# A perceiver block on one core: query weights averaged a head at a time, and a new order of the opening

## The chip, the core and the metric

The kernel runs on one core of one Trainium2 chip. A core has a matrix engine (TensorE, "PE" in the profile; its weight loads are the row "PEld"), a vector engine (DVE), a scalar engine (ACT), GpSimd (POOL) and a synchronisation engine (SP), which here issues nearly all transfers. Each engine takes its own instructions in order, and engines wait for each other through semaphores. TensorE writes to PSUM, a small accumulation memory; the rest of the data lies in SBUF. The metric is the device time of one execution in microseconds, the median of several runs.

## What is computed

A block of three residual layers works on x of shape 32 x 64 x 512 in float32. The change touches only the first layer, cross attention: x is normalised, projected to queries of four heads of 128, rotated by position, and attends to a masked memory of 32 x 1601 x 512 with one shared head of keys and values.

```python
xn = _rmsnorm(_layernorm(x), rms_scale)
mn = _rmsnorm(ctx_1024, rms_scale)
q = einsum('BTD,NDH->BTNH', xn, q_w)
k, v = einsum('BSD,cKDH->cBSKH', mn, kv_w)
q = rope(q, S + arange(T)) * 128 ** -0.5
k = rope(k, arange(S))
probs = softmax(where(mask, q . k, -2.4e38))
x = x + einsum('BTNH,NHD->BTD', probs . v, out_w)
# then causal self attention of 16 heads, and a feed-forward of 2048
```

## The kernel before

**Tiling.** The 2048 tokens are four groups of four tiles of 128 (`GROUPS`, `GQ = 512`). Width 512 is four chunks of 128 (`DC`). A query of group g and head h (`query`, L229) is four products over the chunks, weights `wq[:, c, h]` against the transposed x of the group (`wide(g)`, from the host array `xT`), 512 tokens wide, into one PSUM bank. In float32 each product is two matmul instructions in the profile, so a query has eight.

**How the layer norm is taken out of the product.** The weights are scaled by 1 + rms_scale (`scale1`), and their mean over the width is subtracted; the mean is itself a product with a matrix `each` (scale1 / 512 on all columns). So raw x can be multiplied. The missing standard deviation of each token comes from `spread_of` (L196, statistics of a 128x512 tile of tokens that `fetch_raw` loads), `deviations` (L203, a power on POOL) and `diagonals` (L211, ACT writes four scaled identities into `eye`). `tables(g)` (L222) multiplies ones by `eye` into a PSUM tile `rb` and on DVE makes the group's cosine and sine tables with the deviations in them. `rotate_query` (L234) then takes two ACT copies and three DVE operations of 128x512 and writes `qT_all`.

**The opening (L263 to L379).** It holds group 0 entirely, the statistics and tables of group 1, the means and centring of the query weights (`wmean`, L324 to L348), the scaling of `wkv`, and a ranking of the sequences by how much of their memory is unmasked: the mask ends and a small table come in one transfer `opening`; `mf` is their cast, `count` two products, `halves`, `need`, `key`, `mine`, `rank`, `here` small DVE operations, `placed` four tiny products, and `ints` holds the order and a flag `fits`. `keep_busy(n)` issues n products of ones that nobody reads. `in_order` (L145) ties the instructions of each engine, SP included, to the order in which they are written.

**After the branch on `fits` (L381, L628).** All engines read the flag, so nothing behind it starts before `ints` is written. The common way, `cross_last`, interleaves the queries of groups 1 to 3 (`query_steps`, L244) with the loads of the memory in ranked order (`load_rows`, `load_rest`), with tokens and x of groups 2 and 3, and from group 2 on with the key and value products of pair 0 (`project`, L517, tile `kvp`). PSUM for queries alternates: even heads take a pool of two banks `ps_lg`, odd heads one of two `ps_pt`. Tiles are shared in place: `wide(g)` has two buffers for four groups, `fetch_raw` one buffer for all, so a load waits until the group before has been read. After the queries a loop over pairs of sequences does projection, logits, softmax and output.

Of the kernel before, what the change touches and what calls it, by code (L numbers as in the profile page):

```python
# [18 lines left out]
F32 = mybir.dt.float32  # L19
# [61 lines left out]
def perceiver_kernel(ctx: ExitStack, tc: tile.TileContext, a: dict, out: bass.AP):  # L81
# [83 lines left out]
    turned_probs = wo.rearrange("p h (k q) -> p (h k) q", q=P)  # L165
    ints = const.tile([1, B + 1], I32, name="ints")

    wq = wo.rearrange("p c (h k) -> p c h k", h=NH)
    scale1 = const.tile([P, DC], F32, name="scale1")


# [14 lines left out]
    def fetch_wide(g, queues):  # L186
        for k, queue in enumerate(queues):
            part = slice(k * DC // len(queues), (k + 1) * DC // len(queues))
            queue.dma_start(wide(g)[:, part], a["xT"][:, g, part])
# [27 lines left out]
    def fetch_rotations(pool):  # L217
        qrot = pool.tile([P, 2, T], F32, name="qrot")
        nc.sync.dma_start(qrot, a["qrot"])
        return qrot  # L220
# [8 lines left out]
    def query(g, h, ps):  # L229
        for c in range(DC):  # L230
            nc.tensor.matmul(ps, wq[:, c, h, :], wide(g)[:, c], start=(c == 0), stop=(c == DC - 1))  # L231
        return ps

    def rotate_query(g, h, ps):  # L234

        t = norm.tile([P, D], F32, tag="xn", name=f"qt_{g}_{h}")
        nc.scalar.copy(t[:H], ps[H:])
        nc.scalar.copy(t[H:], ps[:H])
        t = t.rearrange("p (b t) -> p b t", t=T)
        nc.vector.tensor_tensor(turn, ps.rearrange("p (b t) -> p b t", t=T), cosr, ALU.mult)  # L240
        nc.vector.tensor_tensor(t, t, sinr, ALU.mult)
        nc.vector.tensor_tensor(qT_all[:, S8 * g : S8 * (g + 1), h, :], turn, t, ALU.add)

    def query_steps(qrot, psq, psr):  # L244

        for g in range(1, GROUPS):
            more = g + 1 < GROUPS
            for h in range(NH):
                q = query(g, h, psq(h, f"q_{g}_{h}"))
                if h == 0 and g > 1:  # L250
                    tables(g, qrot, psr(f"rb_{g}"))
                rotate_query(g, h, q)
                if more and h < 2:
                    spread_of(g + 1, 2 * h)
                    spread_of(g + 1, 2 * h + 1)
                if more and h == 1:
                    deviations(g + 1)
                if more and h == 2:
                    diagonals(g + 1)
                yield g, h  # L260


    with ExitStack() as st:  # L263
        r1 = st.enter_context(tc.tile_pool(name="r1", bufs=1))
        ps_q = [
            st.enter_context(tc.tile_pool(name=f"ps_q{k}", bufs=2, space=PSUM)) for k in range(2)
        ]
        ps_b = st.enter_context(tc.tile_pool(name="ps_b", bufs=2, space=PSUM))
        ps_r = st.enter_context(tc.tile_pool(name="ps_r", bufs=2, space=PSUM))


        CUTS = np.cumsum([0, B * NC, 4 * B * 5, 4 * 2 * NC])
        opening = r1.tile([P, CUTS[-1]], U8, name="opening")
        m8, table, steps = (opening[:, i:j] for i, j in zip(CUTS, CUTS[1:]))
        table = table[:B].bitcast(F32).rearrange("p (k b) -> p k b", b=B)
        steps = steps[:B].bitcast(F32).rearrange("p (k c) -> p k c", c=NC)

        begin = len(nc.cur_bb.bb.instructions)


        def keep_busy(n):
            idle = ps_b.tile([P, P], F32, tag="b", name=f"idle_{n}")
            for _ in range(n):
                nc.tensor.matmul(idle, ones, ones, start=True, stop=True)

        nc.sync.dma_start(opening, a["opening"])
        nc.scalar.dma_start(scale1, a["rms"])
        for k in (0, 2):
            nc.sync.dma_start(wo[:, k : k + 2], a["wq"][:, k : k + 2])
        keep_busy(5)  # L290
        mf = r1.tile([P, B, NC], F32, name="mf")
        nc.vector.tensor_copy(mf.rearrange("p b c -> p (b c)"), m8)
        nc.vector.tensor_scalar(scale1, scale1, 1.0, None, ALU.add)
        each = r1.tile([P, DC, P], F32, name="each")
        nc.scalar.activation(
            each, scale1.unsqueeze(2).to_broadcast([P, DC, P]), AF.Copy, scale=1.0 / D
        )
        fetch_wide(0, [nc.sync, nc.sync])
        fetch_raw(0)
        qrot = fetch_rotations(r1)  # L300
        nc.sync.dma_start(wkv, a["wkv"])


        halves = r1.tile([B, B, 2, NC], F32, name="halves")
        for k in range(2):
            part = slice(k * T, (k + 1) * T)
            count = ps_r.tile([P, B, NC], F32, tag="r", name=f"count_{k}")
            nc.tensor.matmul(
                count[:B].rearrange("p b c -> p (b c)"),
                ones[part, :B],  # L310
                mf[part].rearrange("p b c -> p (b c)"),
                start=True,
                stop=True,
            )
            nc.vector.scalar_tensor_tensor(
                halves[:, :, k],
                count[:B],
                0.0,
                steps[:, k].unsqueeze(1).to_broadcast([B, B, NC]),
                ALU.is_gt,  # L320
                ALU.mult,
            )
        keep_busy(4)
        wmean = ps_b.tile([P, D], F32, tag="b", name="wmean")  # L324
        for c in range(DC):
            nc.tensor.matmul(wmean, each[:, c], wo[:, c], start=(c == 0), stop=(c == DC - 1))
        need = r1.tile([B, B], F32, name="need")
        nc.vector.tensor_reduce(need, halves.rearrange("p b k c -> p b (k c)"), AX.X, ALU.max)

        key = r1.tile([B, B], F32, name="key")  # L330
        nc.vector.scalar_tensor_tensor(key, need, float(B), table[:, 0], ALU.mult, ALU.add)
        own = r1.tile([B, B], F32, name="own")
        nc.vector.tensor_tensor(own, key, table[:, 1], ALU.mult)
        mine = r1.tile([B, 1], F32, name="mine")
        nc.vector.tensor_reduce(mine, own, AX.X, ALU.add)
        above = r1.tile([B, B], F32, name="above")
        nc.vector.tensor_scalar(above, key, mine, None, ALU.is_gt)
        rank = r1.tile([B, 1], F32, name="rank")
        nc.vector.tensor_reduce(rank, above, AX.X, ALU.add)
        here = r1.tile([B, B], F32, name="here")  # L340
        nc.vector.tensor_scalar(here, table[:, 2], rank, None, ALU.is_equal)
        placed = ps_r.tile([P, 2, B], F32, tag="r", name="placed")
        nc.tensor.matmul(placed[:1, 0], mine, here, start=True, stop=True)
        nc.tensor.matmul(placed[:1, 1], table[:, 3, 0:1], here, start=True, stop=True)
        for c in range(DC):
            nc.vector.scalar_tensor_tensor(  # L346
                wo[:, c], wo[:, c], scale1[:, c : c + 1], wmean, ALU.mult, ALU.subtract
            )  # L348
        heads = [ps_q[h % 2].tile([P, GQ], F32, tag="q", name=f"q_0_{h}") for h in range(NH)]
        query(0, 0, heads[0])  # L350

        fit2 = r1.tile([1, 2, B], F32, name="fit2")
        nc.vector.tensor_tensor(fit2[:, 0], placed[:1, 0], table[:1, 4], ALU.is_lt)
        nc.vector.tensor_scalar(fit2[:, 1], placed[:1, 0], float(B), None, ALU.is_ge)
        fit = r1.tile([1, 1], F32, name="fit")
        nc.vector.tensor_reduce(fit, fit2.rearrange("p k b -> p (k b)"), AX.X, ALU.min)
        nc.vector.tensor_copy(ints[:, :B], placed[:1, 1])
        nc.vector.tensor_copy(ints[:, B:], fit)
        for k in range(4):
            spread_of(0, k)  # L360
        deviations(0)
        diagonals(0)
        for c in range(DC):
            nc.scalar.activation(wkv[:, c], wkv[:, c], AF.Copy, scale=scale1[:, c : c + 1])
        query(0, 1, heads[1])
        fetch_raw(1)
        fetch_wide(1, [nc.sync])
        for k in range(4):
            spread_of(1, k)
        deviations(1)  # L370
        query(0, 2, heads[2])
        tables(0, qrot, ps_b.tile([P, GQ], F32, tag="b", name="rb_0"))
        query(0, 3, heads[3])
        for h in range(NH):
            rotate_query(0, h, heads[h])
            if h == 1:
                diagonals(1)
        tables(1, qrot, ps_b.tile([P, GQ], F32, tag="b", name="rb_1"))
        in_order(begin, (Engine.PE, Engine.DVE, Engine.Activation, Engine.Pool, Engine.SP))  # L379

    fits = nc.values_load(  # L381
# [1338 lines left out]
```

## Time and profile before

| what | value |
|---|---|
| median of 3 runs | 900.34 us (899.08 to 900.46) |
| profiled execution | 899.0 us |
| its span | 896.1 us |
| TensorE busy | 881.9 us, 98% |
| VectorE busy | 626.9 us, 70% |
| ScalarE busy | 377.6 us, 42% |
| first query starts | 10.63 us |
| first query of group 1 starts | 27.5 us |
| first `kvp` product starts | 45.6 us |

The profile is one execution. The span runs from its first to its last recorded instruction; what lies around it is 2.9 us. The page gives busy times by engine, the busy share in forty slices, the chain of work that ended last, groups of instructions by line and shape, and transfers with their time from issue to landing. The timeline lists instructions by start, with the idle time of the engine before them and who ended it in brackets. A busy TensorE is not necessarily one at its peak, since matmuls are pipelined.

### The profile page before, as it was taken

The numbers are of one execution on the slowest core, as the hardware profiler recorded it, in microseconds if no ns is written. First come the engines' busy times: TensorE is split into PE (matmuls) and PEld (weight loads), VectorE is DVE, ScalarE is ACT, GpSimd is POOL, SyncE is SP. The second block draws the span as 40 slices with busy tenths as digits, with TensorE's granted clock in tenths as the row PEclk, the third lists the DMA queues.
The fourth block names the chain that finished last, engine by engine and source line by source line (L and its number), as shares of the span: only waits on it lengthen the run. The fifth ranks groups of instructions, "written<-read, shape, count | busy, mean of one in ns | idle before, by whom it ended". The sixth has DMA issues, their size and how long they took to land.

```text
span 896.1 us, 12923 instructions
## 1 busy us (share of the span) xinstructions
PE 881.9 (98%) x4536; PEld 635.0 (71%) x4536; DVE 626.9 (70%) x1198; ACT 377.6 (42%) x811; POOL 67.3 (8%) x79
## 2 busy tenths in 40 slices
PE   9999999999999999999999999999999999999997
PEld 4456777777778767667666766676668878788885
DVE  5975656455655671688889888885776886876864
ACT  2554545545555431222222323224554554555550
POOL 0110111111101100000000000000001000010000
PEclk9999999999999999999999999999999999999999
DMA  8975898775685342011111100100000020010101
GB/s 267 318 250 182 233 250 261 222 248 159 198 257 157 101 161 101 1 59 40 44 37 48 35 25 25 36 12 1 1 1 1 1 47 1 7 42 1 32 16 52
DMA packets 58723, 88.05 MB, mean 98 GB/s; under 512 B 10516, under 2 KB 30872, under 8 KB 58264
## 3 DMA queue, kind: packets, MB, share of 16 engines
q1 hardware_dynamic: 57888, 86.58, 32.1%
q8 instruction: 38, 0.62, 0.3%
q10 hardware_dynamic: 760, 0.55, 0.2%
q14 instruction: 37, 0.30, 0.1%
HBM read 78.72 MB, written 4.19 MB: 93 GB/s over the span
## 4 chain that ended last, share of the span: by engine, by line
PE 86%; DVE 9%; ACT 2%; issue 1%; DMA 1%; POOL 0%; POOLq 0%; ACTq 0%
PE y L1530 13%; PE kvp L523 13%; PE fh L1179 11%; PE xo L649 6%; PE aV L1268 5%; PE aWQ L1256 5%; PE aWK L1256 5%; PE aout L1377 5%; PE q L231 5%; PE lgp L565 3%; PE enc L633 3%; PE pt L618 2%; PE sc L1311 1%; PE aptp L1350 1%; PE po L1363 1%; DVE s L1316 1%
## 5 line engine op out<-in xcount | busy, mean ns | idle before, releaser
L523 PE MATMUL kvp<-wkv,ct 128*128 128x256 f32 x576 | 134.7, 379 | 0.0
L523 PEld LDWEIGHTS kvp<-wkv,ct 128*128 128x128 f32 x576 | 107.0, 190 | 21.6 <-issue 8.8
L1530 PE MATMUL y<-wp,hTh 128*128 128x512 f32 x236 | 94.4, 400 | 0.4 <-DVE xres L1507 0.4
L1530 PE MATMUL y<-wp,hTl 128*128 128x512 f32 x236 | 92.8, 393 | 0.0
L1179 PE MATMUL fh<-fxh,wf 128*128 128x512 f32 x256 | 71.6, 401 | 1.3 <-DVE mv_f L128 0.9
L1187 ACT ACTIVATE bank<-fh 128x512 f32<-128x512 f32 x64 | 38.2, 597 | 76.9 <-PE fh L1179 76.9
L1179 PE MATMUL fh<-fxl,wf 128*128 128x512 f32 x256 | 70.5, 397 | 0.0
L530 ACT ACTIVATE kv<-kvp,rstd 128x256 f32<-128x256 f32 x72 | 34.1, 474 | 84.0 <-PE kvp L523 84.0
L572 DVE CUSTOM_DVE_ANT_0 pr<-lgp,bias 128x384 f32<-128x384 f32 (+6 forms) x64 | 28.5, 458 | 46.9 <-PE lgp L565 46.6
L1377 PE MATMUL aout<-bank,aoT 128*128 128x512 f32 x128 | 59.2, 605 | 1.1 <-ACT aoT L1371 1.1
L1525 DVE SCALAR_TENSOR_TENSOR hTl<-bank,lnw,hTh 128x512 fp32r<-128x512 f32 x59 | 44.0, 750 | 20.7 <-ACT hTh L1524 20.7
L649 PE MATMUL xo<-wo,encT 128*128 128x512 f32 x128 | 57.7, 594 | 0.2 <-ACT encT L642 0.2
L231 PE MATMUL q<-xres,wo 128*128 128x512 f32 x128 | 56.4, 593 | 0.6 <-DVE wo L346 0.6
L1179 PEld LDWEIGHTS fh<-fxl,wf 128*128 128x128 f32 x256 | 48.3, 189 | 11.2
L1179 PEld LDWEIGHTS fh<-fxh,wf 128*128 128x128 f32 x256 | 46.7, 188 | 13.2 <-issue 2.2
L1530 PEld LDWEIGHTS y<-wp,hTh 128*128 128x128 f32 x236 | 44.3, 188 | 14.0 <-DVE xres L1507 3.4
L1195 DVE TENSOR_TENSOR sums<-sums,bank 128x512 f32<-128x512 f32 x56 | 38.5, 688 | 20.8 <-ACT bank L1187 20.7
L1333 ACT ACTIVATE s<-s 128x1024 f32<-128x1024 f32 x15 | 15.9, 1060 | 86.5 <-DVE s L1326 86.5
L1530 PEld LDWEIGHTS y<-wp,hTl 128*128 128x128 f32 x236 | 44.5, 188 | 10.0
L1355 ACT COPY wo<-aptp 64x256 f32<-64x256 f32 x64 | 23.4, 366 | 66.1 <-PE aptp L1350 48.9
L1268 PE MATMUL aV<-bank,axT 128*128 128x512 f32 x112 | 51.2, 600 | 0.0
L1256 PEld LDWEIGHTS aWQ<-axT,bank 128*128 128x128 f32 x224 | 42.6, 190 | 11.8 <-issue 6.7
(176 smaller groups left out, 1562.9 us busy)
## 6 DMA issues: line engine op xcount, KB each, us to landing
nat<-in_ctx_dram SPq DMA_DIRECT2D x64, 256.0 KB, 4.8
ct<-in_ctxT_dram SPq DMA_DIRECT2D x7, 768.0 KB, 4.5
xres<-in_x_dram SPq DMA_DIRECT2D x8, 512.0 KB, 6.2
xres<-in_x_dram SPq DMA_DIRECT2D x32, 128.0 KB, 4.8
qs<-bank SPq DMA_DIRECT2D x32, 128.0 KB, 3.7
raw_g<-in_W_fcT_dram SPq DMA_DIRECT2D x16, 256.0 KB, 4.1
raw_g<-in_W_projT_dram SPq DMA_DIRECT2D x16, 256.0 KB, 3.8
raw_q<-in_W_fcT_dram SPq DMA_DIRECT2D x16, 256.0 KB, 2.9
```

Of the source, the lines that this page charges most:

```text
L231: nc.tensor.matmul(ps, wq[:, c, h, :], wide(g)[:, c], start=(c == 0), stop=(c == DC - 1))
L523: nc.tensor.matmul(ps.rearrange("p k h -> p (k h)"), cts[p][:, c, j * P : (j + 1) * P], wkv[:, c].rearrange("p k h -> p (k h)"), start=(c ...
L530: nc.scalar.activation(kvs[p][:, j], ps, AF.Copy, scale=rstds[p][:, j : j + 1])
L649: nc.tensor.matmul(o, encT[:, h].rearrange("p s t -> p (s t)"), wo[:, h, :], start=(h == 0), stop=(h == NH - 1),)
L1179: nc.tensor.matmul(ps, wf[:, c, cols], part[:, c, :], start=(i == 0 and c == 0), stop=(i == 1 and c == DC - 1),)
L1187: nc.scalar.activation(g, ps, AF.Gelu)
L1195: nc.vector.tensor_tensor(sums[:, 0], so_far[0], g, ALU.add)
L1256: nc.tensor.matmul(ps[:, m, :], ws[w][:, c, (m0 + m) * P : (m0 + m + 1) * P], xT[:, c, :], start=(c == 0), stop=(c == DC - 1),)
L1268: nc.tensor.matmul(ps, xT[:, c, i * P : (i + 1) * P], ws["WV"][:, c, :], start=(c == 0), stop=(c == DC - 1),)
L1377: nc.tensor.matmul(ps, oT[:, c, :], ws["WO"][:, c, :], start=(c == 0), stop=(c == DC - 1))
L1525: nc.vector.scalar_tensor_tensor(lo, g, w, hi.bitcast(F32), ALU.mult, ALU.subtract)
L1530: nc.tensor.matmul(y, part[:, t, :], wp[:, c, :], start=(c == 0 and i == 0), stop=(c == FC - 1 and i == 1),)
```

## The change

The weight array is stored by head instead of by chunk, so that one head's weights are one transfer. The mean of the weights is made for each head by itself, eight passes of 128x128 in place of a share of eight of 128x512, and centring becomes four 128x128 operations for each head in place of four of 128x512 for all.

The transfers are issued in a new order: head 0's weights, x of group 0, head 1's weights, those of heads 2 and 3, the tokens of group 0, the opening table, x of group 1 (before: only after the tokens of group 1), rotations, `wkv`. The second transfer of tokens follows the statistics of group 0 as before.

On the engines, query (0,0) follows the first mean; the means of heads 1 and 2, query (0,1) and the mean of head 3 come next; VectorE does the statistics of group 0 between centring heads 1, 2 and head 3; then comes the whole ranking, with query (0,2) inside it. The statistics of group 1 stand behind two rotations of group 0 (before: ahead of them), its diagonals behind the third, and its tables after query (1,2), in the branch; queries (1,0) to (1,2) are rotated together after them.

```diff
-    wq = wo.rearrange("p c (h k) -> p c h k", h=NH)
+    wq = wo.rearrange("p h (c k) -> p c h k", c=DC)
...
         for g in range(1, GROUPS):
             more = g + 1 < GROUPS
+            waiting = []
             for h in range(NH):
-                q = query(g, h, psq(h, f"q_{g}_{h}"))
-                if h == 0 and g > 1:
+                waiting.append((h, query(g, h, psq(h, f"q_{g}_{h}"))))
+                if h == (2 if g == 1 else 0):
                     tables(g, qrot, psr(f"rb_{g}"))
-                rotate_query(g, h, q)
+                if h >= 2 or g > 1:
+                    for k, q in waiting:
+                        rotate_query(g, k, q)
+                    waiting.clear()
...
+        nc.scalar.dma_start(scale1, a["rms"])
+        nc.sync.dma_start(wo[:, 0], a["wq"][:, 0])
+        fetch_wide(0, [nc.sync, nc.sync])
+        nc.sync.dma_start(wo[:, 1], a["wq"][:, 1])
+        nc.sync.dma_start(wo[:, 2:], a["wq"][:, 2:])
+        fetch_raw(0)
         nc.sync.dma_start(opening, a["opening"])
-        nc.scalar.dma_start(scale1, a["rms"])
-        for k in (0, 2):
-            nc.sync.dma_start(wo[:, k : k + 2], a["wq"][:, k : k + 2])
-        keep_busy(5)
-        mf = r1.tile([P, B, NC], F32, name="mf")
-        nc.vector.tensor_copy(mf.rearrange("p b c -> p (b c)"), m8)
+        fetch_wide(1, [nc.sync])
+        qrot = fetch_rotations(r1)
+        nc.sync.dma_start(wkv, a["wkv"])
...
-        fetch_wide(0, [nc.sync, nc.sync])
-        fetch_raw(0)
-        qrot = fetch_rotations(r1)
-        nc.sync.dma_start(wkv, a["wkv"])
+        heads = [ps_q[h % 2].tile([P, GQ], F32, tag="q", name=f"q_0_{h}") for h in range(NH)]
+
+        def averaged(h):
+            ps = ps_b.tile([P, HD], F32, tag="b", name=f"wmean_{h}")
+            for c in range(DC):
+                nc.tensor.matmul(
+                    ps, each[:, c], wq[:, c, h], start=(c == 0), stop=(c == DC - 1)
+                )
+            return ps
+
+        def centre(h, ps):
+            for c in range(DC):
+                nc.vector.scalar_tensor_tensor(
+                    wq[:, c, h], wq[:, c, h], scale1[:, c : c + 1], ps, ALU.mult, ALU.subtract
+                )
+
+        keep_busy(6)
+        centre(0, averaged(0))
+        keep_busy(2)
+        query(0, 0, heads[0])
+        means = [averaged(h) for h in (1, 2)]
+        for h in (1, 2):
+            centre(h, means[h - 1])
+        query(0, 1, heads[1])
+        mean = averaged(3)
+        for k in range(4):
+            spread_of(0, k)
+        deviations(0)
+        diagonals(0)
+        centre(3, mean)
+        for c in range(DC):
+            nc.scalar.activation(wkv[:, c], wkv[:, c], AF.Copy, scale=scale1[:, c : c + 1])
+        fetch_raw(1)
+        mf = r1.tile([P, B, NC], F32, name="mf")
+        nc.vector.tensor_copy(mf.rearrange("p b c -> p (b c)"), m8)
...
-        keep_busy(4)
-        wmean = ps_b.tile([P, D], F32, tag="b", name="wmean")
-        for c in range(DC):
-            nc.tensor.matmul(wmean, each[:, c], wo[:, c], start=(c == 0), stop=(c == DC - 1))
...
+        query(0, 2, heads[2])
         placed = ps_r.tile([P, 2, B], F32, tag="r", name="placed")
...
-        for c in range(DC):
-            nc.vector.scalar_tensor_tensor(
-                wo[:, c], wo[:, c], scale1[:, c : c + 1], wmean, ALU.mult, ALU.subtract
-            )
-        heads = [ps_q[h % 2].tile([P, GQ], F32, tag="q", name=f"q_0_{h}") for h in range(NH)]
-        query(0, 0, heads[0])
...
-        for k in range(4):
-            spread_of(0, k)
-        deviations(0)
-        diagonals(0)
-        for c in range(DC):
-            nc.scalar.activation(wkv[:, c], wkv[:, c], AF.Copy, scale=scale1[:, c : c + 1])
-        query(0, 1, heads[1])
-        fetch_raw(1)
-        fetch_wide(1, [nc.sync])
-        for k in range(4):
-            spread_of(1, k)
-        deviations(1)
-        query(0, 2, heads[2])
         tables(0, qrot, ps_b.tile([P, GQ], F32, tag="b", name="rb_0"))
         query(0, 3, heads[3])
         for h in range(NH):
             rotate_query(0, h, heads[h])
             if h == 1:
+                for k in range(4):
+                    spread_of(1, k)
+                deviations(1)
+            if h == 2:
                 diagonals(1)
-        tables(1, qrot, ps_b.tile([P, GQ], F32, tag="b", name="rb_1"))
```

More of the change, by code (lines that the diff above doesn't have):

```diff
@@ L1689 @@
     arrays["xT"] = given["x"].reshape(-1, 4 * P, DC, P).transpose(3, 0, 2, 1)
-    arrays["wq"] = given["L0_xattn_q_w"].reshape(NH, DC, P, HD).transpose(2, 1, 0, 3).reshape(P, DC, D)
+    arrays["wq"] = given["L0_xattn_q_w"].reshape(NH, DC, P, HD).transpose(2, 0, 1, 3).reshape(P, NH, D)
     arrays["wkv"] = given["L0_xattn_kv_w"].reshape(2, DC, P, HD).transpose(2, 1, 0, 3)
```

## The prediction

> **What bounds the kernel now.** I read the page first, then the chain of waits for the first 70 us, then the timeline and the stages of the same stretch, and last the landing of single transfers.
>
> ```profile
> PE 881.9 (98%) x4536; PEld 635.0 (71%) x4536; DVE 626.9 (70%) x1198; ACT 377.6 (42%) x811; POOL 67.3 (8%) x79
> ```
> ```profile
> 16.16 5.87 DMA xres<-in_x_dram
> 25.08 1.29 ACT xres L215 x4
> 26.42 1.12 PE rb L224 x2
> 27.54 17.23 PE q L231 x40
> 44.77 0.86 PE rb L224 x2
> 45.63 1.73 PE kvp L523 x8
> ```
> TensorE is the bound: busy 98%, and from 26.42 us the chain (start, us, what) is PE alone. From 70 to 200 us the list of waits has PE waiting only for its own issue and a few tenths for others. So what counts is when PE reaches a fixed point of its program after the changed part. I take the key product `kvp` of pair 0, behind query (2,0) and the spread `rb_2`: 45.63 us now. A microsecond there is a microsecond at the end. Forty query passes take 17.23 us, 0.43 each; a query (8 passes) is 3.43, an `rb` 0.86.
>
> The timeline of the opening (start, us, engine, line, shape, count, wait in brackets):
> ```profile
> 1.06 2.50 PE L284 MATMUL idle<-ones 128*128 128x128 f32 x10 [1.06 <-DVE neghalf L96]
> 3.50 1.50 PE L308 MATMUL count<-mf,ones 64*32 64x416 f32 x4
> 4.93 1.16 PE L284 MATMUL idle<-ones 128*128 128x128 f32 x8
> 5.92 3.87 PE L326 MATMUL wmean<-wo,each 128*128 128x512 f32 x8
> 9.83 2.72 DVE L346 SCALAR_TENSOR_TENSOR wo<-wo,scale,wmean 128x512 f32<-128x512 f32 x4 [1.31 <-PE wmean L326]
> 10.63 10.57 PE L231 MATMUL q<-xres,wo 128*128 128x512 f32 x24 [0.64 <-DVE wo L346]
> ```
> Ranking, means and centring stand in front of the first query, at 10.63 us; then PE runs on, with one hole before `rb_1` at 26.42. The stage table (length; busy and count of PE, PEld, DVE, ACT, POOL; clock, DMA) shows the second resource:
> ```profile
> 30.00:35.00 5.00, 5.00 (x13) 2.28 (x12) 4.80 (x8) 2.09 (x4) 0.00 (x0) 1.00 1.06 371
> 35.00:40.00 5.00, 5.00 (x13) 2.20 (x12) 4.86 (x10) 4.78 (x12) 0.00 (x0) 1.00 0.99 324
> ```
> ```profile
> 45.66 0.69 DVE L240 TENSOR_TENSOR xres<-q,xres 128x512 f32<-128x512 f32 x1 [1.71 <-PE rb L224]
> ```
> VectorE is nearly full behind PE and catches up only at 45.66. Work pushed back onto it lands in a full stretch.
>
> Landings (KB, us from issue), in the order of issue at 1.20, 2.13 and 2.61 us:
> ```profile
> wo<-in_wq_dram SPq DMA_DIRECT2D x1, 512.0 KB, 4.2
> ...
> xres<-in_xT_dram SPq DMA_DIRECT2D x1, 512.0 KB, 7.0
> ...
> xres<-in_xT_dram SPq DMA_DIRECT2D x1, 512.0 KB, 8.0
> ```
> By bytes issued so far: 0.15 MB (the opening table) down at 3.0 us, 0.67 MB at 5.4, 1.20 at 7.8 (a wait of PE ends there), 1.72 at 9.1, 2.25 at 10.6, then 1.4 us per 0.52 MB. I read the new order of transfers on this curve.
>
> **The change, to the first query.** `wq[0]` is 0.26 MB: down at 3.55. x halves: 0.79 MB at 5.9, 1.31 MB at 8.1. `wq[1]` 8.75, `wq[2:]` 10.2, tokens (`fetch_raw`) 11.6 and 13.0, opening table 13.4, next group's x 16.1, `wkv` 17.7. Twelve idle passes end near 4.0; `each` (rms down at 3.16, then 0.16 on DVE and 0.63 on ACT) is ready at 4.05. A mean is 8 passes of 128x128; the nearest row is the second idle group, 0.136 each (1.09 in all), and the means take 1.1 apiece. Bounds: 0.107 (a quarter of the 512-wide 0.43) and 0.19 (the weight load of the `wmean` passes). `averaged(0)` ends 5.15. One centring operation is 128x128: the 128x512 one is spaced 0.68, and the 128x128 vector rows take 0.28, so 0.28, four 1.1. Query (0,0) starts at 6.1, 4.5 us sooner than before, runs two chunks to 7.8, waits for the second half of x at 8.1 and ends 9.9.
>
> **From there to the ranking.** `averaged(1)`, `(2)` end 11.0 and 12.0, query (0,1) 15.45, `averaged(3)` 16.5. VectorE meanwhile: centre(1), (2) to 13.3; four `spread_of` at 0.66 + 0.18, spaced 0.80, to 16.5; deviations 0.17; centre(3) to 17.8; and only then the cast `mf`, 0.38, to 18.2. The counts stand in PE's queue next and need `mf`: **PE waits 1.75 us**, 16.5 to 18.25, with queries (0,2) and (0,3), whose operands (0,2) already has, queued behind. Counts 1.43 (19.7), query (0,2) 23.15, placed 0.25, `rb_0` 0.86 (24.25), query (0,3) 27.7. The ranking chain on DVE (two counts' comparison 1.07, `need` 1.01, six small operations 1.3) lies under query (0,2). The `fits` load and branch come behind `ints` at 24.15 and lie under query (0,3); uncovered they would cost about the 0.62 gap seen at 27.34 now.
>
> PE thus reaches query (1,0) at 27.7, against 27.54 before; but before had `rb_1` done, which is now 0.86 behind query (1,2). Ready for query (2,0): 27.7 + 13.73 + 0.86 = 42.3, against 41.3. **+1.0 us.** In summary: 4.5 gained at the start; lost again 0.3 to x, 3.3 to three means, 1.43 to counts, 0.25 to placed, 1.75 to `mf`; regained about 1.5 of holes (centring, 0.93 before `rb_1`).
>
> **VectorE behind it.** `tables(0)` follows `rb_0`, 24.3 to 25.5. Rotations at 1.95 each (three 128x512 rows): (0,0), (0,1) to 29.4; then the four spreads of group 1, which before ran in waits, 3.4, to 32.7; (0,2) to 34.6. On ACT `diagonals(1)` (POOL 1.01, then 1.28) holds the copies of (0,3) until 36.3; that rotation ends 37.65, 1.1 late. Spreads of group 2 to 41.05. `tables(1)` to 42.25. Rotation (1,0) reads its query's PSUM by 42.95. Query (2,0) takes that very buffer (even heads alternate over two): **PE waits 0.7.** It ends 46.45. `diagonals(2)` is behind the copies of (1,2), which need the buffer of rotation (1,0), free at 44.15: 45.4 + 1.28 = 46.7, so `rb_2` waits **0.3**. `kvp` starts at 47.6 against 45.63. From there a step has 1.73 of `kvp` more on PE than on DVE, and DVE catches up as it did.
>
> **SP's queue.** Everything of the branch stands behind `ints`, 13.15 before and 24.15 now: `nat` 0 from 19.1 to 26.2, tokens of group 2 (they overwrite what the spreads of group 1 read) from 22.8 to 30.9 and 32.4, x of group 2 from 25.5 to 33.4, `ct` 0 to 34.2, `nat` 1 from 33 to about 39.5. Needed: tokens about 38, landing near 36.5 (3.6 to 6.4 us were seen); x at 42.3, landing 39; `ct` at 47.6, landing 42. The slack of 1.5 to 5 us covers it at no cost; were the tokens 3 us later still, query (2,0) would be 1.5 later. POOL's powers are moved with their spreads and only `diagonals` wait for them, as counted.
>
> **Sum:** +1.0 +0.7 +0.3 = **+2.0 us**. The profiled execution took 899.0, span 896.1 and 2.9 around it; it becomes 901.0. The median of the runs is 1.3 above it, so the forecast is **902.3 us**. About 0.2% (1.8 us) is what a measurement of this kernel can tell from no change, so the value lies just beyond that edge.
>
> **A rule against the change.** The row: idle passes took 0.25 us each before 3.5 us and 0.136 after 4.9, at a printed clock of 1.00 in both. The Trainium skill, "TensorE: Matmul & The Clock Gate" (Part 1), says that the array runs at half rate until it has been busy for a window of about 3.4 us, and again after an idle window of that length. My longest hole is 1.75, so the sum is +2.0; should the hole grow past the window, the page would put the next 3.4 us of matmul work at half rate, an estimate of 1.7 to 3.4 more, sum about +4 to +5. I take the former: holes of 0.8 to 1.2 us in this trace left the next passes at 0.43.
>
> **Rivals.**
> 1. Likeliest: as summed, own range +1.3 to +3.2, chance 0.50, two thirds of it beyond 0.2%.
> 2. VectorE does not hold PE at queries (2,0) and `rb_2`: only +1.0, 901.3. For it: 0.7 and 0.3 are small differences of long sums. Against: 4.8 of 5 us busy already. 0.20.
> 3. More is late: means at 0.19 a pass move query (0,1) and the centring by 0.8; tokens of group 2 landing after 38.5, or the clock, add 1 to 3. +4, 904.3. Against: the idle row and the slack above. 0.20.
> 4. Not slower: the single mechanism is the 1.75 us wait of the counts. If `mf` were cast by 16.5, PE would not wait, DVE would be earlier by as much and the two later holds go too: 2.0 - 1.75 - 1.0 = -0.75, 899.6; with means at 0.107 (0.7 less) and x in time (0.3) it reaches -1.75, and errors of the sum carry some of it beyond 0.2%. It decides from the point where DVE's 13.3 to 18.2 shrinks by 1.0. Against: every row in it is measured but the centring. 0.10, of which 0.06 beyond 0.2%.
> That the first query does not come sooner at all (`wq[0]` down only at 5.4) moves its end by 0.4 and sits in the range.
>
> **Numbers.** Slower by over 0.2%: 0.33 + 0.20 = 0.53; within: 0.17 + 0.20 + 0.04 = 0.41; faster 0.06. The range leaves out the fast end of 4 and the far end of 3: 899.9 to 904.8.
>
> **What would show it.** First query near 6.1 with a wait at its third chunk; a PE hole before the counts near 16.5 to 18.2 put down to `mf`; query (1,0) near 27.7; DVE without gaps from 24 to 50; a wait of query (2,0) on DVE L240; `kvp` near 47.6. Wrong if the hole before the counts is under 0.8 us, or if `kvp` starts before 46.5.

## The result, and the profile after

The changed kernel takes 905.43 us in the median of six runs (901.97 to 906.91), the kernel before 899.60 in six beside it (898.59 to 900.46). The ratio is 1.0062, 95% interval 1.0047 to 1.0077: slower, as forecast, but by 5.8 us where 2.0 were worked out, and outside the range of 899.9 to 904.8.

The profiled execution took 906.87 us, span 905.3, so 9.2 more span than before; its time is only 7.9 more, since 1.6 us lie around the span instead of 2.9. The chain of waits in the changed kernel's first 55 us (start, length in us, what):

```profile
0.75 3.35 DMA scale<-in_rms_dram
...
5.00 2.08 PE wmean L310 x8
7.08 0.85 PE idle L288 x4
7.93 4.38 PE q L231 x8
...
19.84 0.30 DVE mf L340
...
20.18 0.89 PE count L347 x4
...
39.80 0.86 PE rb L224 x2
40.66 3.45 PE q L231 x8
44.10 1.90 issue
46.00 5.37 PE q L231 x8
51.37 0.86 PE rb L224 x2
52.23 1.73 PE kvp L543 x8
```

The fixed point, the first `kvp`, is at 52.23 and was at 45.63: 6.6 us later, 47.6 was forecast. Three lines carry the surprise. The first mean takes 2.08 us for eight passes, and the same eight take 0.9 later. Query (2,0) waits 1.9 us, as "issue", where 0.7 was expected. And its eight passes take 5.37 us instead of 3.43. The stage table (start:end, length, PE busy and count, granted clock, DMA share, GB/s) says why:

```profile
44.00:46.00 2.00, 0.09 (x2) 1.00 1.04 310
46.00:47.00 1.00, 1.00 (x3) 1.00 1.03 401
47.00:48.00 1.00, 1.00 (x3) 0.63 1.08 395
48.00:49.00 1.00, 1.00 (x2) 0.50 1.01 215
49.00:50.00 1.00, 1.00 (x2) 0.50 1.00 264
50.00:51.00 1.00, 1.00 (x3) 0.66 1.06 279
51.00:52.00 1.00, 1.00 (x3) 1.00 1.05 358
```

After the hole TensorE's clock is granted at half for 3.4 us, from 47.3 to 50.7. What holds the query is on VectorE (timeline: start, us, engine, line, shape, and in brackets the idle time before it):

```profile
36.07 0.69 DVE L242 TENSOR_TENSOR bank<-xres,qt 128x512 f32<-128x512 f32 x1
38.47 0.69 DVE L240 TENSOR_TENSOR xres<-q,xres 128x512 f32<-128x512 f32 x1 [1.71 <-ACT qt L238]
...
45.22 0.68 DVE L240 TENSOR_TENSOR xres<-q,xres 128x512 f32<-128x512 f32 x1
```

The L240 at 45.22 reads the PSUM buffer of query (1,0); query (2,0) enters it at 46.00. The 1.71 us at 38.47 are rotation (0,3), waiting for its ScalarE copies.

From `kvp` to 661 us the distance stays at 6.5 to 6.6. There, in the last tile of self attention, comes a second half-rate stretch (661.7 to 665.1); the first `y` product starts at 669.4 against 661.2, 8.2 later. The last 1.0 of the span lies behind the last product.

### The profile page after: what moved, and what is told of

It is laid out like the page before. It is cut to its first block, busy times and chain, and to the rows that moved or that the text cites. A ratio compares the mean times of both kernels' runs of the same rounds, so it can differ in the third digit from the quotient of the medians.

```text
span 905.3 us, 12984 instructions
## 1 busy us (share of the span) xinstructions
PE 887.0 (98%) x4558; PEld 640.5 (71%) x4558; DVE 629.1 (69%) x1210; ACT 376.7 (42%) x811; POOL 67.4 (7%) x79
## 4 chain that ended last, share of the span: by engine, by line
PE 86%; DVE 9%; ACT 2%; issue 1%; DMA 0%; POOL 0%; ACTq 0%; POOLq 0%
PE y L1550 13%; PE kvp L543 13%; PE fh L1199 11%; PE q L231 6%; PE xo L669 6%; PE aV L1288 5%; PE aout L1397 5%; PE aWQ L1276 5%; PE aWK L1276 5%; PE lgp L585 3%; PE enc L653 3%; PE pt L638 2%; PE sc L1331 1%; PE aptp L1370 1%; PE po L1383 1%; DVE s L1336 1%
## 5 line engine op out<-in xcount | busy, mean ns | idle before, releaser
L231 PE MATMUL q<-xres,wo 128*128 128x512 f32 x128 | 59.6, 617 | 1.9 <-issue 1.9
L1550 PEld LDWEIGHTS y<-wp,hTl 128*128 128x128 f32 x236 | 44.5, 188 | 9.9
```

What stands on the lines that cost most here:

```text
L1550: nc.tensor.matmul(y, part[:, t, :], wp[:, c, :], start=(c == 0 and i == 0), stop=(c == FC - 1 and i == 1),)
```

## The experiments

All stand beside runs of the kernel before on the same chip. "kvp" is the start of the first such product on the timeline (45.47 before, 52.06 after), a finer measure than the time, since half-rate stretches come and go between executions; it is that of one profiled execution for each kernel, though, and contains the half rate ahead of it. In the texts written before the runs, "cold" means that the first passes run at half rate, "warm" at full. "First mean" is the length of its eight passes; where a kernel has the old mean, it is that of the eight idle passes before it.

| kernel | first mean | hole before query (2,0) | half rate behind it | kvp | ratio to before, 95% |
|---|---|---|---|---|---|
| before | 1.16 (idle) | 0 | no | 45.47 | 1 |
| after | 2.08 | 1.91 | yes | 52.06 | 1.0062 (1.0047 to 1.0077) |
| e1_fill | 1.16 | filled | no | 48.77 | 1.0056 (1.0036 to 1.0076) |
| e2_rms | 2.04 | 1.90 | yes | 50.34 | 1.0039 (1.0024 to 1.0053) |
| e3_busy8 | 1.16 | 1.91 | yes | 50.42 | 1.0065 (1.0044 to 1.0087) |
| e4_mf | 2.08 | 1.90 | no | 50.03 | 1.0026 (1.0016 to 1.0036) |
| e5_defer_only | 2.07 (idle) | 2.36 | no | 48.17 | 1.0032 (1.0023 to 1.0041) |
| e6_tab_q10 | 1.99 (idle) | 0 | no | 45.88 | 0.9998 (0.9988 to 1.0008) |
| e7_all | 1.13 | filled | no | 47.76 | 1.0029 (1.0017 to 1.0040) |
| e8_fewer_stats | 2.08 | 0 | no | 48.95 | 1.0034 (1.0023 to 1.0046) |
| e9_diag | 2.07 | 0.33 | no | 49.30 | 1.0038 (1.0021 to 1.0055) |
| e10_mended | 1.13 | 0.33 | no | 45.91 | 0.9998 (0.9989 to 1.0006) |
| e11_opening_only | 2.07 | 0; 2.10 before rb_1 | no | 50.99 | 1.0044 (1.0028 to 1.0059) |
| e12_rank_early | 2.07 | 0.61 | no | 46.70 | 1.0012 (1.0005 to 1.0018) |

**Filling the hole.**

```diff
+                if (g, h) == (2, 0):
+                    fill = psr("fill")
+                    for _ in range(9):
+                        nc.tensor.matmul(fill[:, :P], ones, ones, start=True, stop=True)
                 waiting.append((h, query(g, h, psq(h, f"q_{g}_{h}"))))
```

> Eighteen idle passes stand ahead of query (2,0) and need nothing, so TensorE is busy where it had its 1.9 us hole (44.1 to 46.0 us). Theory A (the hole makes the clock gate halve the rate of the passes that follow): granted clock 1.00 from 46 to 52 us, query (2,0) in 3.4 us and not 5.4, kvp near 50.3 and not 52.2, the median 1.5 to 2 us under that of the changed kernel. Theory B (the slow stretch at 47 to 51 us is chance or waits for x of group 2): the clock or the 5.4 us stay, kvp at 52 or later, no gain.

`kvp` came at 48.77, sooner than even theory A said. The stages of this kernel:

```profile
42.00:44.00 2.00, 2.00 (x20) 1.00 0.99 315
44.00:46.00 2.00, 2.00 (x6) 1.00 1.04 382
46.00:48.00 2.00, 1.80 (x5) 1.00 1.01 229
```

The clock stays whole and the query takes its 3.4 us. But 2.1 of the 3.3 us gained have nothing to do with the filling: this execution's first mean ran at full rate, with the same twelve idle passes ahead of it.

```profile
4.96 1.16 PE L314 MATMUL wmean<-wo,each 128*128 128x128 f32 x8 [0.97 <-ACT each L306]
```

The median, 904.38 of only four runs, does not show the gain. What the profile gives is the price with full rate from the first mean to `kvp`: 48.77, **3.3 us behind** before, in this one execution.

**The late scale.**

```diff
-        nc.scalar.dma_start(scale1, a["rms"])
+        nc.sync.dma_start(scale1, a["rms"])
         nc.sync.dma_start(wo[:, 0], a["wq"][:, 0])
```

> The 2 KB transfer of rms_scale goes first on SP's queue, ahead of head 0's weights. Theory A (it landed at 4.09 us[...], and that made the first mean late and cold): it lands near 3.0, the hole of 1.0 us before the first mean shrinks to 0.5 or less, query (0,0) ends 1 to 2 us sooner than 12.3, kvp sooner by as much. Theory B (head 0's weights land later by what the small one gains): query (0,0) ends within 0.3 us of 12.3.

The first mean started at 4.41 instead of 5.00, now waiting for the weights; query (0,0) ended at 10.6 instead of 12.3; `kvp` 1.7 sooner. Theory A. Of it 0.6 is the start, the rest is that the query found full rate. The 1.9 us hole and the half rate behind it stayed.

**More idle passes at the start.**

```diff
-        keep_busy(6)
+        keep_busy(8)
```

> Sixteen idle passes in front of the first mean instead of twelve. Theory A (the hole of 1.0 us before the first mean kept TensorE at half rate until about 9.5 us): full rate from about 5 us, the first mean in 1.0 us and not 2.1, query (0,0) in 3.5 and not 4.4, its end near 10.5, all later points 1.5 to 2 us sooner. Theory B (warm-up is a matter of chance): the passes of the mean stay at 0.26 us and everything is 0.1 us later or the same.

First mean 1.16 us, query (0,0) 3.69, its end 10.7, `kvp` at 50.42, 1.6 sooner: the numbers of theory A. But theory B is not ruled out. e1 had the same 1.16 with twelve passes, and the last section finds that both executions came to full rate at nearly the same moment, 4.6 us. The time, 905.0, did not follow: this profile has the half rate at 45.6 to 49.0 and once more at 660.0 to 663.4.

**The cast and the counts early.**

```diff
+        mf = r1.tile([P, B, NC], F32, name="mf")
+        nc.vector.tensor_copy(mf.rearrange("p b c -> p (b c)"), m8)
         query(0, 1, heads[1])
         mean = averaged(3)
+        counts = []
+        for k in range(2):
+            part = slice(k * T, (k + 1) * T)
+            count = ps_r.tile([P, B, NC], F32, tag="r", name=f"count_{k}")
...
+            counts.append(count)
         for k in range(4):
             spread_of(0, k)
...
-        mf = r1.tile([P, B, NC], F32, name="mf")
-        nc.vector.tensor_copy(mf.rearrange("p b c -> p (b c)"), m8)
```

The count products go with the cast.

> The cast mf and the two count products stand ahead of the statistics of group 0; the rest of the ranking stays where it was. The prediction's rival 4: the 1.75 us wait before query (0,2) goes and both later holds with it, kvp 2.7 us or more sooner than 52.2. Theory A (VectorE's total work between 13 and 46 us is what counts, and this edit takes none of it away): the 1.75 us go, 1.0 of it comes back as a wait of the four tiny placed products for here, and kvp is 0.7 to 1.3 us sooner; the hole before query (2,0) stays at 1.5 us or more.

The 1.75 us wait went; 0.78 came back as a wait of `placed` for `here`; the hole before query (2,0) stayed at 1.90, 0.8 sooner. That is theory A; `kvp` came 2.0 sooner and not 0.7 to 1.3, because no half rate followed the hole in this execution. Rival 4 of the prediction falls: removing PE's wait takes no work off VectorE.

**The deferral alone.** The kernel before, with the statistics of group 1 behind two rotations, its diagonals behind the third, its tables behind query (1,2), and queries (1,0) to (1,2) rotated together after them.

```diff
         fetch_wide(1, [nc.sync])
-        for k in range(4):
-            spread_of(1, k)
-        deviations(1)
...
             rotate_query(0, h, heads[h])
             if h == 1:
-                diagonals(1)
-        tables(1, qrot, ps_b.tile([P, GQ], F32, tag="b", name="rb_1"))
+                for k in range(4):
+                    spread_of(1, k)
+                deviations(1)
+            if h == 2:
+                diagonals(1)
```

> The kernel before, with one part of the change alone: statistics of group 1 behind two rotations, its tables behind query (1,2). Theory A (late ranking and late deferral together fill VectorE; each alone does not): the hole before rb_1 is gone, query (2,0) is held 1.5 to 2 us by DVE L240 and kvp starts at 45.9 to 46.9 (45.63 before), so 0.3 to 1.3 us later, the median within 0.2% of before or just over it. Theory B (the deferral is what costs): kvp at 48 or later, median over 902.

Neither theory. The hold is 2.36 us and `kvp` at 48.17, 2.7 behind before; 0.9 of that is idle passes at half rate ahead of the first query, so the deferral costs some 1.8 us by itself. That "each alone does not" cost was wrong.

**Only the tables of group 1 later.** In the kernel before, `tables(1)` moves behind query (1,0).

```diff
-                if h == 0 and g > 1:
+                if h == 0:
                     tables(g, qrot, psr(f"rb_{g}"))
...
-        tables(1, qrot, ps_b.tile([P, GQ], F32, tag="b", name="rb_1"))
```

> The kernel before, with only the tables of group 1 moved behind query (1,0), as the other groups have them; statistics stay early. Theory A (VectorE sets the pace of this stretch): the 0.93 us hole before rb_1 goes, but most of it comes back as a wait of rb_2 for the diagonals of group 2, kvp 0.1 to 0.5 us sooner than 45.63, time within 0.2%. Theory B (TensorE alone sets it): kvp 0.9 us sooner.

The hole before `rb_1` went and 0.75 us came back before `rb_2`. Same time. Theory A, with `kvp` 0.4 later instead of sooner, because here the idle passes at the start ran at half rate.

**All mends together**: the four edits above on the changed kernel (scale first, cast and counts early, hole filled, and fourteen idle passes where e3 has sixteen).

> The changed kernel with its separate losses mended together: rms first on SP, fourteen idle passes at the start, mf and counts ahead of the statistics, eighteen idle passes in the hole before query (2,0). Theory A (what is left is VectorE's backlog, which none of these takes away): full rate throughout the first 60 us, kvp at 47 to 48.3, still 1.5 to 2.7 us behind before, median 901 to 902.5. Theory B (the clock, the late rms and the wait of the counts were all of it): kvp at 46 or sooner, median level with before.

`kvp` 47.76 at full rate, median 902.03. Theory A: with the clock whole, 2.3 us remain.

**Less work on VectorE.** Three of the four statistics of group 2 are left out.

```diff
+        if g == 2 and k:
+            nc.vector.tensor_copy(mvs[g][:, k], mvs[g][:, 0])
+            return
         nc.vector.bn_stats(st, xres[:, 2 + k])
```

> The changed kernel, with the statistics of three of group 2's four tiles left out (their values are copied from the first tile, so the output is not the reference's): 1.9 us less on VectorE and nothing else less. Theory A (VectorE's backlog holds query (2,0), and the hole brings the half rate): the hole shrinks to 0.3 us or less, no half rate at 44 to 52, kvp at 48.3 to 48.9 after a cold first query and 46.3 to 47 after a warm one. Theory B (the hold has another source, x of group 2 or the buffer itself): hole and kvp stay.

The hole is gone: queries (1,3) and (2,0) run on as sixteen passes without a break, at full clock.

```profile
40.65 7.14 PE L234 MATMUL q<-xres,wo 128*128 128x512 f32 x16
```

`kvp` 48.95 after a slow first mean. Theory A; x of group 2 does not hold the query, and its buffer does so only as long as VectorE has yet to read it.

**The diagonals behind the copies.**

```diff
-            if h == 2:
+            if h == 3:
                 diagonals(1)
```

> The changed kernel with the diagonals of group 1 behind the rotation of (0,3) instead of ahead of it: the same work, but ScalarE makes the copies of (0,3) without waiting for the power and the diagonals. Theory A (1.7 of VectorE's lateness at query (2,0) is this wait of L240): rotation (0,3) starts without its wait of 1.7 us, the hole before query (2,0) is 0.2 to 0.5 us instead of 1.9, no half rate there, kvp at 48.8 to 49.3 after a cold start and 46.8 to 47.3 after a warm one; median 901.5 to 903.5. Theory B (VectorE loses the time elsewhere): the hole stays at 1.5 or more.

The same two L240 rows in this kernel, and PE's:

```profile
36.94 0.69 DVE L240 TENSOR_TENSOR xres<-q,xres 128x512 f32<-128x512 f32 x1
...
43.68 0.68 DVE L240 TENSOR_TENSOR xres<-q,xres 128x512 f32<-128x512 f32 x1
...
44.46 3.67 PE L231 MATMUL q<-xres,wo 128*128 128x512 f32 x8 [0.33 <-PE q L231]
```

No wait at rotation (0,3), query (2,0) held for 0.33 us instead of 1.9, no half rate there; `kvp` 49.30, the upper end of what A gave. The median of five runs, 904.24, is above the expected 903.5; its profile has the half rate at 659 us.

**Mended, with that order.**

```diff
-        nc.scalar.dma_start(scale1, a["rms"])
+        nc.sync.dma_start(scale1, a["rms"])
...
-        keep_busy(6)
+        keep_busy(7)
...
-            if h == 2:
+            if h == 3:
                 diagonals(1)
```

with the cast and counts early, and no filling.

> As the mended kernel before (rms first, fourteen idle passes, mf and counts early), with the diagonals of group 1 behind rotation (0,3) and without the idle passes in front of query (2,0). Theory A (with both waits gone the front alone is left): query (1,0) near 26.3, hole before query (2,0) at most 0.5, kvp at 46.0 to 46.7 when warm, 0.5 to 1.2 behind before, median within 0.2% of before. Theory B: kvp at 47.5 or later as without this edit.

The front of this kernel on PE:

```profile
1.06 3.22 PE L288 MATMUL idle<-ones 128*128 128x128 f32 x14 [1.06 <-DVE neghalf L96]
4.44 1.13 PE L310 MATMUL wmean<-wo,each 128*128 128x128 f32 x8 [0.16 <-DMA wo<-in_wq_dram]
5.41 0.61 PE L288 MATMUL idle<-ones 128*128 128x128 f32 x4
6.01 3.70 PE L231 MATMUL q<-xres,wo 128*128 128x512 f32 x8
...
41.07 3.67 PE L231 MATMUL q<-xres,wo 128*128 128x512 f32 x8 [0.33 <-PE q L231]
```

Query (0,0) starts at 6.01, the prediction's 6.1. `kvp` 45.91, ratio 0.9998: the whole loss is made good, nothing more. Theory A, at its early end. The first mean now waits for head 0's weights, which land near 4.4 us.

**The new opening alone**: the changed kernel with statistics, diagonals, tables and rotations of group 1 where they were.

```diff
+        for k in range(4):
+            spread_of(1, k)
+        deviations(1)
         tables(0, qrot, ps_b.tile([P, GQ], F32, tag="b", name="rb_0"))
...
             if h == 1:
-                for k in range(4):
-                    spread_of(1, k)
-                deviations(1)
-            if h == 2:
                 diagonals(1)
+        tables(1, qrot, ps_b.tile([P, GQ], F32, tag="b", name="rb_1"))
```

> The changed kernel with the new opening, but statistics of group 1 again ahead of the tables of group 0, its diagonals behind the second rotation, its tables ahead of the branch and each rotation behind its query as before. Theory A (the later ranking is what makes VectorE late, and the deferral only moves the wait): TensorE waits about 2 us before rb_1 instead of before query (2,0), kvp at 48 to 49 when warm, 50 to 51 when cold. Theory B (the deferral is the loss): kvp at 46.5 or sooner when warm.

PE waits 2.10 us before `rb_1`, none before query (2,0); `kvp` 50.99 after a slow start. Theory A: with the late ranking the deferral only moves the wait. So each half costs alone, and, once the 1.9 us of half rate behind the hold are set aside, both together cost no more than the opening.

**Ranking to the front again**, in the mended kernel, in VectorE's idle time before the first means.

```diff
+        nc.sync.dma_start(opening, a["opening"])
         nc.sync.dma_start(wo[:, 0], a["wq"][:, 0])
...
+        mf = r1.tile([P, B, NC], F32, name="mf")
+        nc.vector.tensor_copy(mf.rearrange("p b c -> p (b c)"), m8)
...
         centre(0, averaged(0))
         keep_busy(2)
         query(0, 0, heads[0])
+        need = r1.tile([B, B], F32, name="need")
...
         means = [averaged(h) for h in (1, 2)]
...
+        placed = ps_r.tile([P, 2, B], F32, tag="r", name="placed")
```

Counts and `halves` go with `mf`, the rest of the small operations with `need`, `ints` with `placed`. Ten idle passes and the four of the counts stand ahead of the first mean, not fourteen idle ones.

> The mended kernel, with the ranking put back to the front, where VectorE waits for the first means: order of transfers rms, opening table, then head 0's weights, x and the rest as in the change; mf, counts and halves ahead of the first mean, need to here under query (0,0), placed and ints behind the means of heads 1 and 2; averaging by head and the deferral stay. Theory A (the later ranking is what fills VectorE; 4.8 us of its work leave the stretch behind the first query): query (0,0) some 0.8 us later than in the mended kernel (ends near 10.4), query (1,0) near 24.3 and not 26.3, kvp at 43.7 to 44.7 when warm, 1 to 1.8 us ahead of before, median 0.1% to 0.2% under before. Theory B (the first query is held by the larger queue of transfers, and the gain is given back): kvp at 45.5 or later, median level with before.

A miss: `kvp` 46.70, ratio 1.0012. The opening table landed at 3.7 us, the counts ended at 5.7, the mean behind them was slow, and query (0,0) ended at 12.4 instead of 10.4. About 1.4 of these 2.0 us are passes at half rate, which lasted to 9.2 us in this execution, so the profile alone does not condemn the order; the median of 21 runs does not show a gain either. VectorE was then 2.73 us idle before `tables(0)`. At the front the ranking stands in TensorE's way instead of VectorE's.

## Why the prediction was wrong

The direction, the first query's new place and VectorE as what holds query (2,0) were right. The step that failed is the rule weighed against the change: "My longest hole is 1.75, so the sum is +2.0", taken because short holes in the old trace had left the next passes whole. Half rate stood in it at nothing; in the profiled execution it cost 2.1 us at the start and 1.9 behind the hold. The terms, in the profiled execution and at `kvp` (52.2 instead of 47.6, 4.6 us):

- **The start, +1.8.** Query (0,0) ended at 12.3, not 9.9. `each` was forecast for 4.05 from the landing of the scale at 3.16; with larger transfers beside it the 2 KB landed at 4.09, so TensorE stood idle from 4.0 to 5.0, and the mean (2.08, not 1.1), the idle passes and the query's first passes ran at half rate. In e1, with the same late scale but at full rate, the query ended at 10.3. So 0.4 of the 2.4 is lateness and 2.1 is half rate. Behind the query 0.6 net came back: later means took 0.112 a pass instead of 0.136 and the counts 0.89 instead of 1.43, while query (0,2) and `rb_0` took 0.4 more. The weights of head 0 were forecast for 3.55; e2 and e10 have the first mean waiting for them to 4.4.
- **The hold of query (2,0), 1.9 instead of 0.7.** The working had rotation (0,3) held by its copies, but let its first operation go ahead; L240 started only behind both copies, after 1.71 instead of 1.1, and rotations are spaced 2.1 instead of 1.95. The trace of before had both: two rotations in a row, and in the list of waits (us in total, times, longest) the very pair (both below). That VectorE holds the query is shown by e8 (less work, no hold) and e9 (the wait away, hold 0.33). L240 reads the same PSUM tile as the copies, and not what they write; why it waits for them was not tried.

```profile
27.18 0.69 DVE L240 TENSOR_TENSOR xres<-q,xres 128x512 f32<-128x512 f32 x1
...
29.30 0.69 DVE L240 TENSOR_TENSOR xres<-q,xres 128x512 f32<-128x512 f32 x1
...
DVE xres L240 <- ACT qt L238: 4.1, 2, 2.4
```

- **The half rate behind the hold, 1.9 instead of 0.** Rival 3 named the clock, and the rule a hole "past the window". In this execution, as in e2 and e3, 1.9 us were enough. The stretch before `kvp` comes in three of the six kernels with a hole of 1.9 us or more, and in none of the eight without, e1 with its filled hole among them. So it takes a hole, but need not follow one.
- **The wait of rb_2, 0.3**, was not there: the slow query hid it. e1 and e9 show 0.20.

The sum is 1.8 + 1.2 + 1.9 - 0.3 = 4.6. The 1.75 us hole of the counts came to 1.75, and the loads behind `ints` cost nothing, as forecast. The gap of 0.62 at 27.34, read as the branch's, is one between weight loads; TensorE's products ran on. Behind `kvp` the second half-rate stretch added 1.7 in this execution. It is in six of the fourteen profiles here, on old and new orders alike, so it tells nothing of the change; it does blur every median by as much.

Without any half rate the change costs 3.3 us at `kvp` (e1), 1.3 more than forecast, and that is nearly all VectorE's hold. That the rest of the median's 5.8 is half rate at the start and behind the hold is likely, but was not resolved run by run. The granted clock of each run, a mean over its span, points that way: the three slowest runs of the changed kernel (906.5 to 906.9) list 0.993 to 0.995, the other three (902.0 to 904.4) 0.997. Likewise in e5 four runs at 903.8 to 904.0 list 0.993 to 0.995, the other sixteen (901.1 to 902.8) 0.996 to 0.998. One stretch takes 0.0019 off the mean (3.4 us at half in 905). The count stays uncertain, since the stretch behind the last product, which holds no product up, takes up to 0.0026, and the half rate of the first mean is not in the figure.

## What to carry to other kernels

A queue freed on the bounding engine is worth what the next engine in line has to spare: two edits that each looked like work moved into cover filled VectorE, and one group of ScalarE operations written a step too early cost 1.6 us of the hold. Price a hole in TensorE's work twice, by its length and by a half-rate stretch that may follow. Read the old list of waits for the pair that the new order will make last.

## What the runs showed of the hardware

**Behind a hole.** A hole of 1.9 us was followed by 3.4 us at half clock in three of four kernels (after, e2, e3; not e4), holes of 2.36 and 2.10 us were not (e5, e11), and the holes of 1.75 us ahead of the counts never. The Trainium skill, "TensorE: Matmul & The Clock Gate", Part 1, has a free-running window of 3.413 us. The profiles agree: each stretch within the work lasts 3.4, and in all seven profiles that have one there and another behind the last product, the starts are whole numbers of windows apart. In the changed kernel they are 47.27, 661.67 and 900.60, so 180 and 70 windows.

So any stretch tells where the windows of its execution lie. In the three cases the hole lies wholly within one (43.9 to 47.3; 41.0 to 44.5; 42.2 to 45.6), which leaves 1.5 us of products in it. In e4 and e11 two windows share the hole, 1.15 and 0.75 us, 1.06 and 1.04. That fits, but e5 does not: 1.92 of its 2.36 us lie in one window, 41.4 to 44.8, and the clock stayed whole. What tips it near 1.9 us stays open. The page's advice in "Why this matters for your kernels", to keep holes under about 3 us, was not enough here: 1.9 sufficed.

**Near 660 us.** Four `spread` products, with four rows of weights, take 2.0 us there. The half rate comes in the six profiles in which a window that they fall in holds at most 1.36 us of other products, and not in the eight in which each such window holds at least 1.49. It looks as if these narrow products hardly count as work; no run changed them.

**At the start.** Twelve idle passes left the first mean slow in six of seven kernels; fourteen or sixteen left it fast in all three. The printed clock reads 1.00 in both, so the length of a pass has to tell; the clock record in the trace begins only with the full rate, at 9.72 us in the changed kernel. In these ten kernels full rate came at the end of the first window with 2.77 us of products or more; with 2.58 or less it did not. Where the first mean took 2.0 us or more, a window ended at 2.9 to 3.6 us, too soon after the first pass at 1.06, and in five of these six kernels the next window contains the idle 1.0 us before the first mean. Where it took 1.2 or less, a window ended at 4.0 to 4.6, e1 with twelve passes at 4.64 and e3 with sixteen at 4.61. So where the windows fell accounts for all ten, and that more passes help is not shown.
